# Attention over a graph: one merged exponential for each pair of tiles, scores in batches of three and five, x loaded in pieces

## The chip, the cores and the metric

The kernel runs on one core of a Trainium2 chip. The core has a matrix engine (PE, with its weight loads shown as PEld), a vector engine (DVE), a scalar engine (ACT), a general engine (POOL) and a queue engine that issues most transfers (SP). Matmul results go to a memory called PSUM, which this kernel uses as eight banks of 512 float32 columns. The metric is the device time of one launch in microseconds (us).

## The reference

Four graph layers run on x (3327 nodes, 128 features) and a 0/1 adjacency matrix adj (3327 x 3327). Each layer normalises, applies relu and adds its result to x. Cut to the layer that takes most of the time:

```python
h = jnp.maximum(_layernorm(x, axis=-1), 0.0)
q = (x @ Wq.T).reshape(d, n, h)      # x is h above; d = 128 heads, n = 3327 nodes, h = 8 elements
k = (x @ Wk.T).reshape(d, n, h)
v = (x @ Wv.T).reshape(d, n, h)
a = jnp.einsum('dnh,dmh->dnm', q, k) * scale
a = a + spatial_encoding + edge_encoding          # both are adj
a = jax.nn.softmax(a, axis=2)
out = jnp.einsum('dnm,dmh->dnh', a, v)
out = out.reshape(n, h * d)
return out @ Wo.T
```

So for each of 128 heads there are 3327 x 3327 scores of eight-element products, 2 adj is added, and the exponential of every score is needed: 1.4 thousand million exponentials. Layer 0 multiplies by adj twice, layer 2 is a gated unit on adj @ h, layer 3 picks nearest neighbours; all that lies outside the attention loop takes 1299 us of the span.

## The kernel before

**Tiling of the attention loop.** Query nodes lie in seven chunks of 476 columns (the last is shorter), key nodes in 26 tiles of 128 partitions (node = partition x 26 + tile), heads in 32 groups of four. A step is one key tile of one (chunk, group); there are 7 x 32 = 224 groups and 5824 steps. Two steps, an even tile and an odd tile, share one buffer `p8` of eight places of 476 columns, so there are 2912 pairs.

**One step, before (`scores`, lines 536 to 557).** Four score matmuls (line 547), one per head, each on its own 32 partitions of the array (their operands lie at partitions 32 i). The letters of `WAYS` (line 505) say how 2 adj reaches each score:

- D: the scores go to an "early" bank (four in turn), and DVE adds the tile of 2 adj while it copies them to `p8` (line 552).
- I: the scores go to a "late" bank, and a second matmul, of an identity with the tile of 2 adj (line 550), adds it in PSUM.
- G: the scores go to a late bank; ACT takes their exponential and POOL multiplies it by exp(2 adj), which is held for odd tiles (line 555).

The even tile is DDDI and the odd tile DDIG. ACT takes the exponential straight from the late banks (line 553): of one place in an even step and of two in an odd step. After the odd step it takes the exponential of the five D places of the pair at once, in place (line 557). PSUM is full: one bank for the accumulator, four early, one for `late1` and two for `late2`.

**Weighing (`weigh`, lines 559 to 576).** Four steps later (`ahead = 4`), four float32 matmuls, each in two passes, multiply the values (9 columns per head, the ninth being 1 for the softmax sum) by the exponentials and accumulate in `acc` (line 564). The four heads use four column groups of the array. After tile 25 DVE copies `acc` out (line 573), and the next group's first weighing may start after that.

**Order.** The loop stands under a manual schedule: each engine runs its instructions in the order of the program text. So PE runs scores, identity, weighing, step by step. A step also holds other work: at tile 4 the loads of the next group's heads on SP (`load_heads`, line 392), from tile 13 the casts of the keys on POOL (`key_pair`, line 414), and during the first chunk the parting of keys and queries into high and low parts on POOL (`Parting.at`). In the last group of a chunk ACT also takes the exponentials of the next chunk's adj tiles (`exp_of`). Outside this loop a planner orders instructions by costs of its own, so the order there need not be that of the text.

**Stage before the loop (lines 421 to 500).** For 26 blocks of nodes, q, k and v are projected on PE, copied by ACT to staging tiles and stored to DRAM from SP. Between blocks one entry of the list `early` runs (lines 444 to 457, line 478): parting of groups 0 and 1, all loads of the first heads in one entry, the exponentials for the first chunk in one entry, then two key casts in each entry. The staging tile of v comes from a pool of four and POOL writes a 1 into the ninth column before every use (line 473).

**Start.** x is loaded into `xs` (partition p holds nodes 26 p to 26 p + 25, called slots) by three transfers of whole rows, the split being in partitions (lines 95 to 98). The first layer norm works in three pieces of slots: `CUTS` (line 134) gives 0 to 4, 4 to 13 and 13 to 26.

Of the kernel before, what the change touches and what calls it, by code (L numbers as in the profile page):

```python
# [8 lines left out]
F32 = mybir.dt.float32  # L9
# [6 lines left out]
AF = mybir.ActivationFunctionType  # L16
# [33 lines left out]
def dram(ap, offset, dims):  # L50
    return bass.AP(tensor=ap.tensor, offset=ap.offset + offset, ap=dims)
# [3 lines left out]
def kernel(  # L55
# [38 lines left out]

    xs = const.tile([P, T, D], F32, name="xs")
    nc.vector.memset(xs[96:P, T - 1, :], 0.0)
    for p0, p1, n in ROW_PARTS:
        nc.sync.dma_start(xs[p0:p1, :n], dram(x_in, p0 * T * D, [[T * D, p1 - p0], [D, n], [1, D]]))

    weights = const  # L100

# [26 lines left out]
    def inv_sqrt(pool, src, name, scale=1.0, bias=0.0):  # L128
# [1 line left out]
        nc.scalar.activation(r, src, AF.Sqrt, bias=bias, scale=scale)  # L130
        nc.vector.reciprocal(r, r)
        return r

    CUTS = (0, T // 6, T // 2, T)

    def in_pieces(f, cuts=CUTS):

# [207 lines left out]
    def exp_of(a2, c):  # L345
        e = e_pool.tile([P, QW], F32, name="e")
        nc.scalar.activation(e[:, : even(c)], a2[:, : even(c)], AF.Exp)
        return e
# [40 lines left out]
                if t == 11:  # L389
                    self.store(side)  # L390

    def load_heads(c, g):
        q0, w = q_chunks[c]
        k_in = kq.tile([P, NP], F32, name="k_in", bufs=1)
        q4 = kq.tile([P, QW], F32R, name="q4")
        v4 = kq.tile([P, 4, T, EA], F32, name="v4")
        nc.gpsimd.memset(k_in[:, N:], 0.0)
        if w % 2:
            nc.gpsimd.memset(q4[:, w : w + 1].bitcast(F32), 0.0)
        for i in range(4):  # L400
            n0 = (4 * g + i) * N
            for j in range(2):
                r = 32 * i + HL * j
                nc.sync.dma_start(k_in[r : r + HL, :N], kt[:, n0 : n0 + N])
                nc.sync.dma_start(q4[r : r + HL, :w].bitcast(F32), dram(qt, E * j * GP + n0 + q0, [[0, 2], [GP, E], [1, w]]))
        for i in range(4):
            n0 = (4 * g + i) * N
            nc.sync.dma_start(
                v4[:, i].rearrange("p t e -> p (t e)"),
                vd[n0 : n0 + NP, :].rearrange("(p t) e -> p (t e)", t=T),  # L410
            )
        return k_in, q4, v4, []

    def key_pair(heads):
# [7 lines left out]
    with tc.tile_pool(name="l1", bufs=1) as pool, tc.tile_pool(name="l1_ps", bufs=3, space=PSUM) as ps:  # L422
# [22 lines left out]
        for g in range(2):  # L445
            part = Parting(g)
            for side in range(2):
                early.append(lambda part=part: (part.load(0), part.load(1)) if part.lo[0] is None else None)
                early.append(lambda part=part, side=side: [part.part(side, i) for i in range(4)] and part.store(side))
        first, e_first = [], []  # L450
        early.append(lambda: first.extend(load_heads(0, 0)))
        ahead_part = Parting(2)
        early.append(lambda: (ahead_part.load(0), ahead_part.load(1)))
        early.append(lambda: e_first.extend(exp_of(a, 0) for a in a_first[1::2]))
        early += [lambda: (key_pair(first), key_pair(first))] * (T // 4)
        if T // 2 % 2:
            early.append(lambda: key_pair(first))
        for r in range(T):
            kp = rows_of(r)
            lhs = hT[:, r * P : r * P + kp]  # L460
            for i, (dst, mx) in enumerate(((qf, q_max), (kf, k_max))):
                pp = ps.tile([P, 2, 512], F32, name="pp", bufs=2)
                for c in range(2):
                    nc.tensor.matmul(pp[:kp, c, :], lhs, w_st[:, i, c * 512 : c * 512 + 512], start=True, stop=True)
                s = st.tile([P, E * NH], F32, name="qk_st")
                nc.scalar.activation(s[:kp], pp[:kp].rearrange("p a b -> p (a b)"), AF.Copy, scale=D**-0.5 if i == 0 else 1.0)
                nc.vector.tensor_reduce(mx[:kp, r : r + 1], s[:kp], AX.X, ALU.max, apply_absolute_value=True)
                store(dst[:E].rearrange("e (r c) -> r e c", c=NH), s.rearrange("p (e c) -> p e c", c=NH), r, kp)
            pp = ps.tile([P, 2, 512], F32, name="pp", bufs=2)
            for c in range(2):  # L470
                nc.tensor.matmul(pp[:kp, c, :], lhs, w_st[:, 2, c * 512 : c * 512 + 512], start=True, stop=True)
            s = st.tile([P, NH, EA], F32, name="v_st")
            nc.gpsimd.memset(s[:, :, E : E + 1], 1.0)
            nc.scalar.copy(s[:kp, :, :E], pp[:kp].rearrange("p a (c e) -> p (a c) e", e=E))
            store(vd.rearrange("(r c) e -> r (c e)", c=NH), s.rearrange("p c e -> p (c e)"), r, kp)

            if r > 1 and early:
                early.pop(0)()
# [23 lines left out]

    WAYS = ("DDDI", "DDIG")
    PLACES = ((0, 1, 2, 5), (3, 4, 6, 7))
    two_i = const.tile([P, P], BF16, name="two_i")
    nc.vector.tensor_copy(two_i, ident)
    engines = {
# [9 lines left out]
    with tc.tile_pool(name="at_in", bufs=1) as a_pool, tc.tile_pool(name="at_p", bufs=3) as p_pool, tc.tile_pool(  # L519
# [13 lines left out]
            q0, w = q_chunks[c]  # L533
            nc.sync.dma_start(adj16[t][:, q0 : q0 + w], a2[:, :w])

        def scores(step, heads, a2, e_a, p8):
            c, _, t = step
            we = even(c)
            _, q4, _, pairs = heads
            ways, places = WAYS[t % 2], PLACES[t % 2]  # L540
            n_d = ways.count("D")
            late = ps.tile([P, 4 - n_d, 512], F32, name=f"late{4 - n_d}")
            early = [ps.tile([P, 512], F32, name="early", bufs=4) for _ in range(n_d)]
            for i in (*range(n_d, 4), *range(n_d)):
                r = slice(32 * i, 32 * i + 32)
                sp = early[i] if i < n_d else late[:, i - n_d]
                nc.tensor.matmul(sp[:, :we], pairs[t // 2][r, t % 2, :], q4[r, :we], start=True, stop=ways[i] != "I")  # L547
            for i in range(4):
                if ways[i] == "I":
                    nc.tensor.matmul(late[:, i - n_d, :we], two_i, a2[:, :we], start=False, stop=True)  # L550
            for i in range(n_d):
                nc.vector.tensor_tensor(p8[:, places[i], :we], early[i][:, :we], a2[:, :we], op=ALU.add)  # L552
            nc.scalar.activation(p8[:, places[n_d] : places[3] + 1, :we], late[:, :, :we], AF.Exp)  # L553
            if ways[3] == "G":
                nc.gpsimd.tensor_tensor(p8[:, places[3], :we], p8[:, places[3], :we], e_a[:, :we], op=ALU.mult)  # L555
            if t % 2:
                nc.scalar.activation(p8[:, :5, :we], p8[:, :5, :we], AF.Exp)  # L557

        def weigh(step, v4, p8):
            c, g, t = step  # L560
# [17 lines left out]
        with tc.manual_schedule(engines=engines):  # L578
# [7 lines left out]
            for j, step in enumerate(steps):  # L586
                c, g, t = step
                n = c * n_groups + g + 1
                more = n < len(groups)
                if t == 0 and j:  # L590
                    heads = coming
                    if g == 0:
                        a_t, a_next = a_next, []
                        e_t, e_next = e_next, []
                if t % 2 == 0:
                    p8 = p_pool.tile([P, 8, QW], F32, name="p8")
                scores(step, heads, a_t[t], e_t[t // 2], p8)
                begun[j] = (step, heads[2], p8)
                if j >= ahead:
                    weigh(*begun.pop(j - ahead))  # L600
                if t == min(4, T // 2) and more:
                    coming = load_heads(*groups[n])
                if c == 0 and g + 2 < n_groups:
                    if t == 0:
                        parting = ahead_part
                    for due in range(t, t + 1 if t < T - 1 else max(T, 16)):
                        parting.at(due)
                        if due == 15 and g + 3 < n_groups:
                            ahead_part = Parting(g + 3)
                            ahead_part.load(0)  # L610
                            ahead_part.load(1)

                if t >= T // 2 and more:
                    key_pair(coming)
                if t == min(6, T // 2) and c + 1 < len(q_chunks):
                    for _ in range(min(len(to_store), 1 + T // n_groups)):
                        store_adj(*to_store.pop(0))
                    a_in = [load_adj(c + 1, i) for i in range(len(a_next), T * (g + 1) // n_groups)]
                if t == max(T - 4, 3) and c + 1 < len(q_chunks):
                    for a, i, w in a_in:  # L620
                        a_next.append(doubled(adj_pools[(c + 1) % 2], a[: rows_of(i), :w], i, w))
                        to_store.append((c + 1, i, a_next[-1]))
                if t % 2 and g == n_groups - 1 and c + 1 < len(q_chunks):
                    e_next.append(exp_of(a_next[t], c + 1))
# [485 lines left out]
```

## Time and profile before

| | us |
|---|---|
| median of the runs (lowest, highest) | 11189.97 (11184.46, 11197.54) |
| the profiled execution's own time | 11195.14 |
| its span, first to last instruction | 11193.4 |
| PE busy | 10850.5 |
| ACT busy | 10199.3 |
| DVE busy | 9343.1 |
| POOL busy | 6016.3 |
| the attention loop, first to last exponential | 576.2 to 10470.6 |

A group line of the profile names the source line, engine, operation, what is written and read with its shape, and the count. After the first bar come the busy time in all and the mean in ns of one. After the second come the idle time of that engine just before these instructions and what ended most of it. Busy times of ACT and PE hold overlaps: an instruction is counted [...] while the next has already started. Where it matters the distance between starts is used; starts are taken from the trace's single records. A row of the timeline gives the start, the time covered, the engine, line and operation, and x for how many were merged into the row. In the table of stages each engine has its busy time with the count of instructions, then come the clock granted to PE, the share of the DMA engines and GB/s.

### The profile page before, as it was taken

How to read it: one execution, taken by the hardware profiler on the slowest of the kernel's cores; microseconds unless marked ns; L12 is line 12 of the kernel's file. 1: busy time of each engine (PE TensorE's matmuls, PEld its weight loads, DVE VectorE, ACT ScalarE, POOL GpSimd, SP SyncE). 2: the span in 40 equal slices, each digit the busy share in tenths (PEclk: the TensorE clock that was granted, in tenths of full speed). 3: DMA queues.
4: the chain of work that ended last, by engine and by line, in shares of the span. 5: the costliest groups of instructions: out<-in, count | busy, mean ns of one | idle time of the engine just before them, and what ended most of it. 6: DMA issues, size and time to landing. Idle time of an engine off the chain costs nothing. (4 is left out here: it accounts for less than half of the span.)

```text
span 11193.4 us, 209350 instructions
## 1 busy us (share of the span) xinstructions
PE 10850.5 (97%) x79530; PEld 3005.9 (27%) x79530; DVE 9343.1 (83%) x15429; ACT 10199.3 (91%) x9152; POOL 6016.3 (54%) x6964
## 2 busy tenths in 40 slices
PE   9899999999999999999999999999999999999996
PEld 4322222222222222222222222222222222222453
DVE  8588888888888888888888888888888888888656
ACT  0399999999999999999999999999999999999522
POOL 0277777555555555555555555555555555555203
PEclk9899999999999999999999999999999999999998
DMA  7755554333333333333333333333333332333432
GB/s 264 238 129 120 123 127 109 65 64 64 68 64 62 67 66 63 68 65 61 68 66 63 66 66 61 67 66 61 66 66 61 66 63 55 61 58 58 135 113 97
DMA packets 417541, 942.25 MB, mean 84 GB/s; under 512 B 67936, under 2 KB 345937, under 8 KB 380940
## 3 DMA queue, kind: packets, MB, share of 16 engines
q1 hardware_dynamic: 412762, 918.98, 37.4%
q8 instruction: 627, 10.27, 0.4%
q0 software_dynamic: 3760, 9.78, 0.3%
q14 instruction: 392, 3.21, 0.1%
HBM read 788.78 MB, written 139.71 MB: 83 GB/s over the span
## 5 line engine op out<-in xcount | busy, mean ns | idle before, releaser
L552 DVE TENSOR_TENSOR p<-early,a 128x476 f32<-128x476 f32 (+1 forms) x14560 | 8426.4, 646 | 1369.4 <-PE early L547 1297.5
L557 ACT ACTIVATE p<-p 128x2380 f32<-128x2380 f32 (+1 forms) x2912 | 7568.4, 2599 | 0.4
L564 PE MATMUL acc<-p,v 128*9 128x476 f32 (+1 forms) x46592 | 5748.5, 564 | 15.3 <-ACT p L557 1.4
L553 ACT ACTIVATE p<-late 128x476 f32<-128x476 f32 (+1 forms) x5824 | 5315.4, 1175 | 13.8 <-DMA q<-qt 10.2
L555 POOL TENSOR_TENSOR p<-p,e 128x476 f32<-128x476 f32 (+1 forms) x2912 | 3528.1, 1212 | 3204.3 <-ACT p L553 2998.6
L547 PE MATMUL late<-q,k 32*128 32x476 f32 (+1 forms) x8736 | 2798.2, 478 | 99.5 <-ACT p L553 39.7
L547 PE MATMUL early<-q,k 32*128 32x476 f32 (+1 forms) x14560 | 2843.6, 478 | 9.4 <-DVE p L552 9.4
L419 POOL CAST k<-k_in 128x256 fp32r<-128x256 f32 x2912 | 1936.5, 697 | 886.4 <-DMA k_in<-kt 339.4
L547 PEld LDWEIGHTS late<-q,k 32*128 32x128 f32 x8736 | 1065.4, 181 | 4890.4 <-ACT p L553 4186.2
L550 PE MATMUL late<-a,two_i 128*128 128x476 bf16 (+1 forms) x5824 | 2180.8, 374 | 0.0
L547 PEld LDWEIGHTS early<-q,k 32*128 32x128 f32 x14560 | 1113.0, 181 | 9.9 <-DVE p L552 9.9
L564 PEld LDWEIGHTS acc<-p,v 128*9 128x9 f32 x46592 | 695.2, 88 | 1272.6 <-issue 1185.8
L550 PEld LDWEIGHTS <-two_i 128*128 128x128 bf16 x5824 | 556.2, 96 | 1329.0 <-issue 1329.0
L189 ACT COPY agg<-agg_ps 128x512 f32<-128x512 f32 x15 | 8.2, 591 | 485.5 <-PE agg_ps L204 290.6
L230 PE MATMUL agg_ps<-a,part 128*128 128x512 bf16 (+1 forms) x1092 | 227.0, 369 | 4.3 <-ACT agg L928 3.2
L272 POOL TENSOR_SCALAR a<-a_in 128x476 bf16<-128x476 f32 (+2 forms) x156 | 221.1, 1417 | 0.5
L272 POOL TENSOR_SCALAR a<-a 128x476 bf16<-128x476 f32 (+1 forms) x26 | 36.4, 1400 | 288.1 <-DMA a<-in_adjT_dram 288.1
L923 PE MATMUL sp<-yT,hT 128*128 128x512 f32 (+1 forms) x364 | 170.7, 610 | 12.3 <-ACT agg L928 6.4
L204 PE MATMUL agg_ps<-a,h 128*128 128x512 f32 (+2 forms) x364 | 148.2, 570 | 26.2 <-DVE h L164 26.2
L573 DVE COPY o<-acc 105x476 f32<-105x476 f32 (+1 forms) x224 | 144.5, 645 | 4.6 <-PE acc L564 4.6
L204 PE MATMUL agg_ps<-a,x 128*128 128x512 f32 (+2 forms) x364 | 145.3, 562 | 0.6 <-ACT x L318 0.6
L230 PEld LDWEIGHTS <-part 128*128 128x128 f16 x1092 | 108.6, 99 | 117.7 <-issue 10.3
(236 smaller groups left out, 2592.0 us busy)
## 6 DMA issues: line engine op xcount, KB each, us to landing
k_in<-kt SPq DMA_DIRECT2D x1792, 207.9 KB
v<-vd SPq DMA_DIRECT2D x896, 117.0 KB
a<-in_adjT_dram SPq DMA_DIRECT2D x50, 1663.5 KB
a<-adj SPq DMA_DIRECT2D x78, 831.8 KB
q<-qt SPq DMA_DIRECT2D x1536, 29.8 KB
a_in<-in_adjT_dram SPq DMA_DIRECT2D x125, 238.0 KB
adj<-a SPq DMA_DIRECT2D x156, 119.0 KB
vd<-v_st SPq DMA_DIRECT2D x25, 576.0 KB
```

What stands on the lines that cost most here:

```text
L204: nc.tensor.matmul(acc[c][:, :w], lhs[:kp, t, :], a[:kp, c0 : c0 + w], start=(t == 0), stop=(t == T - 1))
L230: nc.tensor.matmul(acc[c][:, :w], part[:, t, :], a[:, c0 : c0 + w], start=(t == 0 and i == 0), stop=(t == T - 1 and i == len(parts) - 1),)
L272: nc.gpsimd.tensor_scalar(a2[:kp, :w], a, 2.0, None, op0=ALU.mult)
L419: nc.gpsimd.tensor_copy(k, slots(k_in)[:, t : t + 2, :])
L547: nc.tensor.matmul(sp[:, :we], pairs[t // 2][r, t % 2, :], q4[r, :we], start=True, stop=ways[i] != "I")
L550: nc.tensor.matmul(late[:, i - n_d, :we], two_i, a2[:, :we], start=False, stop=True)
L552: nc.vector.tensor_tensor(p8[:, places[i], :we], early[i][:, :we], a2[:, :we], op=ALU.add)
L553: nc.scalar.activation(p8[:, places[n_d] : places[3] + 1, :we], late[:, :, :we], AF.Exp)
L555: nc.gpsimd.tensor_tensor(p8[:, places[3], :we], p8[:, places[3], :we], e_a[:, :we], op=ALU.mult)
L557: nc.scalar.activation(p8[:, :5, :we], p8[:, :5, :we], AF.Exp)
L564: nc.tensor.matmul(acc[32 * i : 32 * i + EA, :w], v4[:kp, i, t, :], p8[:kp, PLACES[t % 2][i], :w], start=(t == 0), stop=(t == T - 1),)
L923: nc.tensor.matmul(sp[:, c0 : c0 + w], slots(zT)[:, t, :], z2T[:, cols], start=True, stop=False)
```

## The change

In the attention loop, `scores` is called once for a pair, at the even tile. Its eight score matmuls go out in two batches: heads 1, 2 and 3 of the even tile; then, after the weighing of an earlier even tile, head 0 of the even tile and heads 2, 3, 1 and 0 of the odd tile. Both identity matmuls follow the second batch. The one I place of the even tile is now head 0, and the three late places lie together in one tile of three banks, so that one activation takes their exponential (1428 columns); the exponential of the five D places follows it. In the odd step POOL multiplies (`times_e`), and the odd tile of the earlier pair is weighed.

Before the loop, the first heads' loads are split into eight pieces: four load keys and queries and run in entries of their own, four load values and run in the entries that cast keys, where the exponentials of the first chunk now stand as well. The four staging tiles of v are fixed ones, and their ninth column is set once.

At the start, x is loaded in three pieces of slots, eight transfers in all.

```diff
-    for p0, p1, n in ROW_PARTS:
-        nc.sync.dma_start(xs[p0:p1, :n], dram(x_in, p0 * T * D, [[T * D, p1 - p0], [D, n], [1, D]]))
+    CUTS = (0, T // 6, T // 2, T)
+    for t0, t1 in zip(CUTS, CUTS[1:]):
+        for p0, p1, n in ROW_PARTS:
+            m = min(t1, n) - t0
+            if m > 0:
+                nc.sync.dma_start(xs[p0:p1, t0 : t0 + m], dram(x_in, (p0 * T + t0) * D, [[T * D, p1 - p0], [D, m], [1, D]]))
...
-        first, e_first = [], []
-        early.append(lambda: first.extend(load_heads(0, 0)))
         ahead_part = Parting(2)
         early.append(lambda: (ahead_part.load(0), ahead_part.load(1)))
-        early.append(lambda: e_first.extend(exp_of(a, 0) for a in a_first[1::2]))
-        early += [lambda: (key_pair(first), key_pair(first))] * (T // 4)
-        if T // 2 % 2:
-            early.append(lambda: key_pair(first))
+        pieces, e_first = [], []
+        first = load_heads(0, 0, pieces)
+        early += pieces[:4]
+
+        key_steps = -(-(T // 2) // 2)
+        for i in range(key_steps):
+
+            def step(i=i):
+                for f in pieces[4 + i : 5 + i if i < key_steps - 1 else None]:
+                    f()
+                for n in (2 * i, 2 * i + 1):
+                    if n < T // 2:
+                        key_pair(first)
+                        e_first.append(exp_of(a_first[2 * n + 1], 0))
+
+            early.append(step)
+        v_sts = [st.tile([P, NH, EA], F32, name=f"v_st{i}", bufs=1) for i in range(4)]
+        for s in v_sts:
+            nc.gpsimd.memset(s[:, :, E : E + 1], 1.0)
...
-            s = st.tile([P, NH, EA], F32, name="v_st")
-            nc.gpsimd.memset(s[:, :, E : E + 1], 1.0)
+            s = v_sts[r % 4]
...
-    WAYS = ("DDDI", "DDIG")
-    PLACES = ((0, 1, 2, 5), (3, 4, 6, 7))
+    WAYS = ("IDDD", "DDIG")
+    PLACES = ((5, 0, 1, 2), (3, 4, 6, 7))
+
+    BATCHES = (((0, 1), (0, 2), (0, 3)), ((0, 0), (1, 2), (1, 3), (1, 1), (1, 0)))
...
+        def scores(step, heads, a2s, between):
+
+            c, _, t = step
+            we = even(c)
+            _, q4, _, pairs = heads
+            p8 = p_pool.tile([P, 8, QW], F32, name="p8")
+            late = ps.tile([P, 3, 512], F32, name="late")
+            for n, batch in enumerate(BATCHES):
+                if n == 1:
+                    between()
+                for odd, i in batch:
+                    way, place = WAYS[odd][i], PLACES[odd][i]
+                    sp = ps.tile([P, 512], F32, name="early", bufs=4) if way == "D" else late[:, place - 5]
+                    r = slice(32 * i, 32 * i + 32)
+                    nc.tensor.matmul(sp[:, :we], pairs[t // 2][r, odd, :], q4[r, :we], start=True, stop=way != "I")
+                    if way == "D":
+                        nc.vector.tensor_tensor(p8[:, place, :we], sp[:, :we], a2s[odd][:, :we], op=ALU.add)
+            for odd, i in BATCHES[1]:
+                if WAYS[odd][i] == "I":
+                    nc.tensor.matmul(late[:, PLACES[odd][i] - 5, :we], two_i, a2s[odd][:, :we], start=False, stop=True)
+            nc.scalar.activation(p8[:, 5:, :we], late[:, :, :we], AF.Exp)
+            nc.scalar.activation(p8[:, :5, :we], p8[:, :5, :we], AF.Exp)
+            return p8
+
+        def times_e(step, p8, e_a):
+            we = even(step[0])
+            assert WAYS[1][3] == "G"
+            nc.gpsimd.tensor_tensor(p8[:, PLACES[1][3], :we], p8[:, PLACES[1][3], :we], e_a[:, :we], op=ALU.mult)
...
                 if t % 2 == 0:
-                    p8 = p_pool.tile([P, 8, QW], F32, name="p8")
-                scores(step, heads, a_t[t], e_t[t // 2], p8)
+                    p8 = scores(step, heads, a_t[t : t + 2], lambda: weigh(*begun.pop(j - ahead)) if j >= ahead else None)
+                else:
+                    times_e(step, p8, e_t[t // 2])
+                    if j >= ahead:
+                        weigh(*begun.pop(j - ahead))
                 begun[j] = (step, heads[2], p8)
-                if j >= ahead:
-                    weigh(*begun.pop(j - ahead))
```

More of the change, by code (lines that the diff above doesn't have):

```diff
@@ L132, in inv_sqrt @@
         return r
-    CUTS = (0, T // 6, T // 2, T)
     def in_pieces(f, cuts=CUTS):
@@ L390, in at, with load_heads @@
                     self.store(side)
-    def load_heads(c, g):
+    def load_heads(c, g, pieces=None):
         q0, w = q_chunks[c]
@@ L399, in load_heads, with scored @@
             nc.gpsimd.memset(q4[:, w : w + 1].bitcast(F32), 0.0)
-        for i in range(4):
+        def scored(i):
             n0 = (4 * g + i) * N
@@ L405, in load_heads, with weighted @@
                 nc.sync.dma_start(q4[r : r + HL, :w].bitcast(F32), dram(qt, E * j * GP + n0 + q0, [[0, 2], [GP, E], [1, w]]))
-        for i in range(4):
+        def weighted(i):
             n0 = (4 * g + i) * N
@@ L411, in load_heads @@
             )
+        for f in (scored, weighted):
+            for i in range(4):
+                if pieces is None:
+                    f(i)
+                else:
+                    pieces.append(lambda f=f, i=i: f(i))
         return k_in, q4, v4, []
@@ L447 @@
             for side in range(2):
-                early.append(lambda part=part: (part.load(0), part.load(1)) if part.lo[0] is None else None)
+                if side == 0:
+                    early.append(lambda part=part: (part.load(0), part.load(1)))
                 early.append(lambda part=part, side=side: [part.part(side, i) for i in range(4)] and part.store(side))
-        first, e_first = [], []
-        early.append(lambda: first.extend(load_heads(0, 0)))
         ahead_part = Parting(2)
         early.append(lambda: (ahead_part.load(0), ahead_part.load(1)))
-        early.append(lambda: e_first.extend(exp_of(a, 0) for a in a_first[1::2]))
-        early += [lambda: (key_pair(first), key_pair(first))] * (T // 4)
-        if T // 2 % 2:
-            early.append(lambda: key_pair(first))
+        pieces, e_first = [], []
[14 more added lines that the diff above has]
+            nc.gpsimd.memset(s[:, :, E : E + 1], 1.0)
         for r in range(T):
@@ L534, in store_adj @@
             nc.sync.dma_start(adj16[t][:, q0 : q0 + w], a2[:, :w])
-        def scores(step, heads, a2, e_a, p8):
+        def scores(step, heads, a2s, between):
             c, _, t = step
@@ L539, in scores @@
             _, q4, _, pairs = heads
[L540 to L555, printed above, removed]
@@ L556, in scores @@
-            if t % 2:
-                nc.scalar.activation(p8[:, :5, :we], p8[:, :5, :we], AF.Exp)
+            p8 = p_pool.tile([P, 8, QW], F32, name="p8")
[10 more added lines that the diff above has]
+                        nc.vector.tensor_tensor(p8[:, place, :we], sp[:, :we], a2s[odd][:, :we], op=ALU.add)
@@ L595 @@
                 if t % 2 == 0:
-                    p8 = p_pool.tile([P, 8, QW], F32, name="p8")
-                scores(step, heads, a_t[t], e_t[t // 2], p8)
+                    p8 = scores(step, heads, a_t[t : t + 2], lambda: weigh(*begun.pop(j - ahead)) if j >= ahead else None)
+                else:
+                    times_e(step, p8, e_t[t // 2])
+                    if j >= ahead:
+                        weigh(*begun.pop(j - ahead))
                 begun[j] = (step, heads[2], p8)
-                if j >= ahead:
-                    weigh(*begun.pop(j - ahead))
                 if t == min(4, T // 2) and more:
```

## The prediction

> **What bounds the kernel now.** I read the page first, then the stages, then the attention loop one instruction at a time.
>
> ```profile
> PE 10850.5 (97%) x79530; PEld 3005.9 (27%) x79530; DVE 9343.1 (83%) x15429; ACT 10199.3 (91%) x9152; POOL 6016.3 (54%) x6964
> ...
> L552 DVE TENSOR_TENSOR p<-early,a 128x476 f32<-128x476 f32 (+1 forms) x14560 | 8426.4, 646 | 1369.4 <-PE early L547 1297.5
> L557 ACT ACTIVATE p<-p 128x2380 f32<-128x2380 f32 (+1 forms) x2912 | 7568.4, 2599 | 0.4
> L564 PE MATMUL acc<-p,v 128*9 128x476 f32 (+1 forms) x46592 | 5748.5, 564 | 15.3 <-ACT p L557 1.4
> L553 ACT ACTIVATE p<-late 128x476 f32<-128x476 f32 (+1 forms) x5824 | 5315.4, 1175 | 13.8 <-DMA q<-qt 10.2
> L547 PEld LDWEIGHTS late<-q,k 32*128 32x128 f32 x8736 | 1065.4, 181 | 4890.4 <-ACT p L553 4186.2
> ```
>
> Two engines look full. The stage table separates them: in the middle of the loop ACT has no gap.
>
> ```profile
> 4000.00:6000.00 2000.00, 1978.30 (x15305) 486.30 (x15301) 1726.38 (x2988) 2000.00 (x1780) 1127.07 (x1258) 1.00 0.34 65
> ```
>
> Here the columns are PE, PEld, DVE, ACT, POOL. PE's busy time is no verdict, because ends are modelled; starts tell more. The timeline of ACT, then of PE:
>
> ```profile
> 5003.34 1.79 ACT L553 ACTIVATE p<-late 128x476 f32<-128x476 f32 x2
> 5004.63 2.57 ACT L557 ACTIVATE p<-p 128x2380 f32<-128x2380 f32 x1
> 5006.71 1.80 ACT L553 ACTIVATE p<-late 128x476 f32<-128x476 f32 x2
> ```
> ```profile
> 5004.40 0.48 PE L547 MATMUL late<-q,k 32*128 32x476 f32 x1
> ...
> 5004.81 0.37 PE L550 MATMUL late<-a,two_i 128*128 128x476 bf16 x1
> 5005.12 0.99 PE L564 MATMUL acc<-p,v 128*9 128x476 f32 x8
> 5006.03 0.48 PE L547 MATMUL late<-q,k 32*128 32x476 f32 x2
> ```
>
> One pair of tiles takes ACT 6.71 - 3.34 = 3.37 us. Over the loop the mean steps from start to start are 0.448 us (one late row of 476), 0.854 (two, 952; median 0.844) and 2.083 (the five, 2380), together 3.384. With the slope between the first two, 0.396/476 = 0.832 ns an element, each instruction costs its elements and only 0.05 to 0.10 us more: the durations 0.996, 1.403 and 2.626 overlap. 2912 pairs x 3.384 + 78 exponentials of the next chunk x 0.488 = 9892 us, against 9894 from first to last exponential (576.2 to 10470.6). So ACT sets the loop.
>
> PE comes close behind. Medians of its starts: scores to identity 0.419, identity to weighing 0.305, weighing to the next scores 0.917, so 1.641 per tile or 3.282 per pair. The tile following an odd one starts 1.743 later: 0.10 us of waiting for ACT per pair. That 0.10 is all the cover PE has.
>
> **What the skill says.** The Trainium skill, "ScalarE: Activation LUTs", What ACT_TABLE_LOAD costs: an activation with immediates takes 186 ns + 0.833 N, and neighbours overlap by 93 ns, so one instruction fewer would be worth some 93 ns. The trace agrees on the slope, but the two late ones show only 0.05. "TensorEngine Tiling (Array Packing)", Key Properties: changing the tiling mode drains TensorE, while separate tiles run in parallel. The trace agrees: four score matmuls start within 0.010 us, and each switch of shape leaves about 0.1 us beyond streaming. "TensorE: Matmul & The Clock Gate", LDWEIGHTS: columns / 1.2 ns, so 107 ns for 128 columns. This fits the 0.419: 0.010 of dispatch, 0.107 weight load in the open after the switch, 476 columns 0.200 (L230's matmuls of 512 columns start 0.216 apart), about 0.102 drain. The same page, Part 3, says weight loads overlap a running matmul only where the row group differs. This trace shows otherwise for L927:
>
> ```profile
> 10839.14 0.12 PEld L927 LDWEIGHTS <-one_rows 3*128 3x128 bf16 x6 [0.23 <-issue]
> 10839.14 0.61 PE L927 MATMUL sp<-n_rows,one_rows 3*128 3x512 bf16 x6
> ```
>
> Six weight loads lie within 0.12 us, though these are two rounds on the same three row groups; the second round's matmuls start 0.227 after the first (10839.143, 10839.370), which is 512 columns (0.213) and little else.
>
> **The change, part by part.**
>
> *Merged exponential.* ACT loses one start per pair: 0.448 + 0.854 become 1428 x 0.8333 + 0.05 = 1.240, plus 0.010 of present waits. ACT's pair becomes 1.250 + 2.083 = 3.333, a saving of 0.051, or 149 us over 2912 pairs if ACT stayed the bound.
>
> *Batches of three and five.* The eight scores and two identity products of a pair (L550, x5824, one per tile) remain, the identities now back to back. The order on PE is: three scores (even heads 1 to 3), weigh, five scores, two identities, weigh. The five are four row groups and then a fifth, odd head 0, on the group of even head 0, so it streams after it. New sum, in start-to-start steps:
> - three scores to weighing: 0.419 less two dispatch steps of 0.0035 = 0.412. The switch from 32-row straight to 9-column shape is in no row; I price it as the one to the identity. Bounds 0.30 (weights loaded ahead, no drain beyond 0.1) to 0.45.
> - weighing to the five: 0.917.
> - five scores to identity: 0.107 + 0.200 + 0.200 + 0.010 + 0.099 = 0.616, with the fifth's weights loaded under the first, as at L927. If not, 0.723.
> - two identities: 0.305 + 0.200 = 0.505; the second needs no switch.
> - weighing: 0.917.
>
> Together 3.367, against 3.282 before: the added serial pass costs more than the merged identity switch returns. PE's 3.367 now lies above ACT's 3.333, so PE becomes the bound and its own waits count in full.
>
> *Where a group of 26 tiles begins.* The accumulator is copied out by DVE after tile 25 is weighed, and the next group's first weighing waits for it.
>
> ```profile
> 5007.86 0.64 DVE L573 COPY o<-acc 105x476 f32<-105x476 f32 x1
> ...
> 5008.12 0.38 PE L550 MATMUL late<-a,two_i 128*128 128x476 bf16 x1
> ...
> 5008.55 0.12 PEld L564 LDWEIGHTS acc<-p,v 128*9 128x9 f32 x8 [0.34 <-DVE o L573]
> ```
>
> Today scores and identity (0.724) lie between; PE loses 5008.55 - 5008.12 - 0.305 = 0.13 of its cover. Then only three scores (0.412) lie between. Last pass at 0.43 after the weighing's start, modelled end 0.99, about 0.08 to DVE, copy 0.64, 0.05 back: 1.77 against 0.917 + 0.412 = 1.33, so 0.44 us. Queued behind: both batches' scores, hence the adds and the exponentials. The first tile of a group also staggers its scores on the new heads' loads (+0.185, median of groups); I keep that (0 if those waits are taken ahead).
>
> A group: 13 x 3.367 + 0.44 + 0.185 = 44.40, against 44.14 measured now. In the 6 of 224 groups that carry 13 extra exponentials ACT stays the bound and gains 13 x 0.051 = 0.7. Loop: 218 x 0.26 - 4 = +53.
>
> *POOL's multiplication* moves to the odd step, before that tile's weighing, in the same order on POOL. It must be done two pairs later (6.7 us) and takes 1.21. *Adds on DVE*: five of 0.56 start to start, 2.8 of 3.37. Both cost nothing; the cover is 0.5 us per pair on DVE.
>
> *Heads in pieces, value buffers set once.* The projection stage stalls around the first load of heads:
>
> ```profile
> 477.08 1.01 ACT L474 COPY v_st<-pp 128x1024 f32<-128x1024 f32 x1 [2.41 <-PE pp L471]
> 496.17 1.02 ACT L466 ACTIVATE qk_st<-pp 128x1024 f32<-128x1024 f32 x1 [18.07 <-DMA qf<-qk_st]
> ```
>
> SP stands in 16 head loads and 4 value loads from 471 to 491 while the stores of results queue behind. Spread over eleven row blocks, each 4 loads cost SP about 2 us per 5.15 us block, and POOL's casts no longer hold the value buffers' memsets. The DMA engines are full (share 1.0) after 500 us and 0.85 to 0.9 before, so at most 15 us come back; I take -10 (bounds -18 to +5).
>
> *x in pieces.* Eight issues for three, about 0.4 us each on SP, under a transfer of 1.7 MB. DVE's first reduction waits elsewhere:
>
> ```profile
> 12.60 0.28 POOL masks.py:199 TENSOR_SCALAR_AFFINE_SELECT ident<-ident 128x128 f32<-128x128 f32 x1 [10.49 <-issue]
> ...
> 12.91 0.23 DVE L508 CAST two_i<-ident 128x128 bf16<-128x128 f32 x1 [11.43 <-POOL ident masks.py:199]
> ```
>
> The cast stands ahead of it on DVE. I take 0; -8 if the planner now puts the layer norm first, +2 if adj's loads start later.
>
> Sum: +53 - 10 = +43 on the span of 11193.4; the profiled run was 11195.1 and the median of the runs is 11190, so 11233.
>
> **Rivals.**
> - *The fifth score shows its weight load.* For it: the skill's sentence. Against: L927. Price 0.107 x 2834 pairs = +303: 11536.
> - *The new switch is cheap, ACT stays the bound (faster).* The place is three scores to weighing. For: never seen, may load weights early; against: every switch in the trace costs about 0.1. Break-even with today is a pair of 3.352, only 0.015 below my sum; below 3.344 it is faster. Below 3.285 ACT decides, for the full -149 - 10: 11031.
> - *A tie at today's time.* The stagger at group starts is taken ahead and the switch is 0.005 cheaper: about 11190.
>
> **How the numbers follow.** Forecast 0.60 (of it 0.05 faster, 0.15 within, 0.40 slower; own range 11160 to 11310), weight load in the open 0.13, cheap switch 0.22, tie 0.05. 0.2% is 22 us, about what a measurement of this kernel can tell from no change. Faster 0.05 + 0.22 = 0.27; same 0.15 + 0.05 = 0.20; slower 0.40 + 0.13 = 0.53. Range 11070 to 11380: it leaves out the open weight load and the far end of the cheap switch.
>
> **What would show it.** Right: PE's starts between even-tile scores 3.36 to 3.40 apart, 0.6 from first of the five to the identity, ACT with small gaps before the late exponential, 128x1428, started 1.24 before the five's. Wrong: ACT without gaps at 3.33 (cheap switch), or 0.72 and more in the five (open load or slower passes); a first layer norm before 12 us.

## The result, and the profile after

The changed kernel takes 11281.08 us (median; 11280.3 to 11284.58) against 11189.22 for the kernel before: a ratio of 1.0082, 95% interval 1.0066 to 1.0098, so 0.8% slower. The forecast was 11233, slower, with 11070 to 11380 as its range.

The profiled spans, 11193.4 and 11280.1, split as follows (us):

| stage | before | after | difference |
|---|---|---|---|
| start to the first exponential of five | 579.1 | 566.9 | -12.2 |
| attention loop, first to last exponential of five | 9891.5 | 9994.7 | +103.3 |
| all after it | 722.8 | 718.5 | -4.3 |

The code of the last stage is the same in both. It took 716.3 to 723.0 in the ten experiments, so 4 us are no more than it varies from run to run.

The page of the changed kernel, parts 1, 4 and 5:

```profile
PE 10972.7 (97%) x79530; PEld 3043.5 (27%) x79530; DVE 9357.5 (83%) x15429; ACT 10188.3 (90%) x6240; POOL 6011.7 (53%) x6942
...
PE 89%; ACT 5%; DVE 2%; issue 2%; DMA 1%; POOL 1%; SPq 0%; DVEq 0%; ACTq 0%; POOLq 0%
...
L584 ACT ACTIVATE p<-p 128x2380 f32<-128x2380 f32 (+1 forms) x2912 | 6348.7, 2180 | 0.0
...
L583 ACT ACTIVATE p<-late 128x1428 f32<-128x1428 f32 (+1 forms) x2912 | 3965.8, 1362 | 129.4 <-PE late L582 122.8
```

ACT lost 2912 instructions (9152 to 6240) and now has gaps before the late exponential, where it waits for PE's identity: 129 us in all, where it had 14. The exponentials of the five are recorded with 2180 ns on the mean instead of 2599 although they do the same work. Records of ACT are longer in the kernel before, where its loop has no gaps, so its busy total (10199 to 10188) does not show the saving. The chain that ended last is PE for 89% of the span. For the kernel before the same view held only the last microseconds and named no engine above 0%.

ACT's timeline, and PE's, in the middle of the loop:

```profile
5003.49 1.36 ACT L583 ACTIVATE p<-late 128x1428 f32<-128x1428 f32 x1
5004.75 2.18 ACT L584 ACTIVATE p<-p 128x2380 f32<-128x2380 f32 x1
5006.87 1.36 ACT L583 ACTIVATE p<-late 128x1428 f32<-128x1428 f32 x1
```
```profile
5004.22 0.49 PE L577 MATMUL early<-q,k 32*128 32x476 f32 x3
5004.64 0.99 PE L597 MATMUL acc<-p,v 128*9 128x476 f32 x8
5005.56 0.48 PE L577 MATMUL late<-q,k 32*128 32x476 f32 x3
5005.56 0.68 PE L577 MATMUL early<-q,k 32*128 32x476 f32 x2
5006.18 0.57 PE L582 MATMUL late<-a,two_i 128*128 128x476 bf16 x2
5006.68 0.99 PE L597 MATMUL acc<-p,v 128*9 128x476 f32 x8
5007.60 0.49 PE L577 MATMUL early<-q,k 32*128 32x476 f32 x3
```

The pair takes PE 7.60 - 4.22 = 3.38 us. The row of two early scores covers 0.68, where a row of scores that run side by side covers 0.48 or 0.49: the fifth score starts 0.322 (median) after the first of its batch.

The timeline at the start of a group:

```profile
5041.47 0.48 PE L577 MATMUL early<-q,k 32*128 32x476 f32 x3
5041.63 0.65 DVE L606 COPY o<-acc 105x476 f32<-105x476 f32 x1
...
5042.34 0.22 PEld L597 LDWEIGHTS acc<-p,v 128*9 128x9 f32 x8 [0.69 <-DVE o L606]
...
5043.35 0.19 PEld L577 LDWEIGHTS late<-q,k 32*128 32x128 f32 x3 [0.80 <-issue]
```

From the three scores to the weighing it takes 0.87 us instead of 0.42, and the next scores follow the weighing after 1.01 instead of 0.92: together 0.55 us a group. Before, such a group began with a wait of 0.13, and that was inside PE's slack.

The timelines at the start of the program:

```profile
3.68 0.69 DVE L159 TENSOR_REDUCE ln_mean<-xs 128x4 f32<-128x512 f32 x1 [2.19 <-DMA xs<-in_x_dram]
...
14.09 19.00 PE L206 MATMUL agg_ps<-a,h 128*128 128x512 f32 x42 [14.09 <-DVE ln_mean L159]
37.61 22.63 PE L206 MATMUL agg_ps<-a,h 128*128 128x512 f32 x50 [4.53 <-DMA a<-in_adjT_dram]
```

The planner now puts the first piece of the layer norm ahead of the cast that waits for POOL. PE starts 12 us earlier (14.09 for 26.16), then waits 4.5 us for adj: the fourth tile is loaded only when DVE, which is in the layer norm's later pieces until then, has released the first of three buffers (its copy from there ends at 31.20, SP issues the load at 31.27). At the end of the first layer 6.0 of the 12 us are left (ACT's first copy of the second product at 334.88 instead of 340.90); the projection stage adds 6.2.

### The profile page after: what moved, and what is told of

Same layout as the page of the kernel before. It is cut to its first block, busy times and chain, and to the rows that moved or that the text cites. A ratio compares the mean times of both kernels' runs of the same rounds, so it can differ in the third digit from the quotient of the medians.

```text
span 11280.1 us, 206623 instructions
## 1 busy us (share of the span) xinstructions
PE 10972.7 (97%) x79530; PEld 3043.5 (27%) x79530; DVE 9357.5 (83%) x15429; ACT 10188.3 (90%) x6240; POOL 6011.7 (53%) x6942
## 4 chain that ended last, share of the span: by engine, by line
PE 89%; ACT 5%; DVE 2%; issue 2%; DMA 1%; POOL 1%; SPq 0%; DVEq 0%; ACTq 0%; POOLq 0%
PE acc L597 45%; PE early L577 15%; PE late L582 12%; PE late L577 10%; PE agg_ps L206 2%; ACT p L584 2%; ACT p L583 2%; PE agg_ps L232 1%; DVE o L606 1%; PE pp L490 1%; DMA qf<-qk_st 0%; POOL rows L988 0%; ACT e L349 0%; PE yp L772 0%; PE pp L497 0%
## 5 line engine op out<-in xcount | busy, mean ns | idle before, releaser
L584 ACT ACTIVATE p<-p 128x2380 f32<-128x2380 f32 (+1 forms) x2912 | 6348.7, 2180 | 0.0
L583 ACT ACTIVATE p<-late 128x1428 f32<-128x1428 f32 (+1 forms) x2912 | 3965.8, 1362 | 129.4 <-PE late L582 122.8
L577 PE MATMUL early<-q,k 32*128 32x476 f32 (+1 forms) x14560 | 3414.1, 457 | 11.4 <-DVE p L579 10.3
L577 PEld LDWEIGHTS early<-q,k 32*128 32x128 f32 x14560 | 1372.5, 182 | 2334.6 <-DVE p L579 2329.1
L582 PE MATMUL late<-a,two_i 128*128 128x476 bf16 (+1 forms) x5824 | 1675.1, 369 | 0.0
L577 PE MATMUL late<-q,k 32*128 32x476 f32 (+1 forms) x8736 | 1415.8, 479 | 22.6 <-ACT p L583 22.5
L577 PEld LDWEIGHTS late<-q,k 32*128 32x128 f32 x8736 | 547.3, 181 | 2345.8 <-ACT p L583 2168.1
L582 PEld LDWEIGHTS <-two_i 128*128 128x128 bf16 x5824 | 330.7, 97 | 965.0 <-issue 965.0
```

Of the source, the lines that this page charges most:

```text
L577: nc.tensor.matmul(sp[:, :we], pairs[t // 2][r, odd, :], q4[r, :we], start=True, stop=way != "I")
L582: nc.tensor.matmul(late[:, PLACES[odd][i] - 5, :we], two_i, a2s[odd][:, :we], start=False, stop=True)
L583: nc.scalar.activation(p8[:, 5:, :we], late[:, :, :we], AF.Exp)
```

## The experiments

Theory: PE has become the bound of the loop, by the serial fifth score and the wait at group starts; what the merge saves on ACT cannot be used. Rivals: the part ahead of the loop disturbs the loop; ACT is still the bound; the loss lies in the wait at group starts alone. All diffs are against the changed kernel, and cut. In the expectations TensorE is PE, VectorE is DVE, ScalarE is ACT and GpSimd is POOL.

**The two halves of the change apart.** First the loop of before, whole, with the new part ahead of it:

```diff
-    WAYS = ("IDDD", "DDIG")
-    PLACES = ((5, 0, 1, 2), (3, 4, 6, 7))
-    BATCHES = (((0, 1), (0, 2), (0, 3)), ((0, 0), (1, 2), (1, 3), (1, 1), (1, 0)))
+    WAYS = ("DDDI", "DDIG")
+    PLACES = ((0, 1, 2, 5), (3, 4, 6, 7))
...
-            nc.scalar.activation(p8[:, 5:, :we], late[:, :, :we], AF.Exp)
+            nc.scalar.activation(p8[:, places[n_d] : places[3] + 1, :we], late[:, :, :we], AF.Exp)
```

> The loop of before with all that the change does ahead of it (x in pieces, heads in pieces, value buffers set once). Theory: the first exponential of five came at 566.9 us instead of 579.1 in the changed kernel, and the loop of before keeps its 3.398 us per pair, so some 12 us less than before: 11177 (11170 to 11182). Rival: the earlier start is lost again in the loop's first groups, which wait for parted keys: 11189.

Measured 11176.82, ratio 0.9991 (0.9982 to 0.9999) to before; first exponential of five at 566.0 and 3.396 us a pair. Then the reverse, the new loop with all that is ahead of it as before (x, the heads' loads and the value tiles):

```diff
-    CUTS = (0, T // 6, T // 2, T)
-    for t0, t1 in zip(CUTS, CUTS[1:]):
-        for p0, p1, n in ROW_PARTS:
...
+    for p0, p1, n in ROW_PARTS:
+        nc.sync.dma_start(xs[p0:p1, :n], dram(x_in, p0 * T * D, [[T * D, p1 - p0], [D, n], [1, D]]))
...
-        first = load_heads(0, 0, pieces)
...
+        early.append(lambda: first.extend(load_heads(0, 0)))
```

> The loop of after with the head of before. Theory: the loss is all in the loop (103 us from the first to the last exponential of five), so about 12 us more than the changed kernel: 11293 (11285 to 11300). Rival: moving loads and casts ahead of the loop disturbed the loop, and it runs like before without them: 11190.

Measured 11290.75, ratio 1.0093 (1.0077 to 1.0108); loop 9992.6, as in the changed kernel. The loss is all in the loop, and the rest of the change gains some 10 us: 11.4 from the kernel before to the first of these runs, 9.7 from the second to the changed kernel.

**The fifth score left out.** Odd head 0 is not computed; its add reads head 1's scores.

```diff
+                    fifth = (odd, i) == (1, 0)
+                    if not fifth:
-                    sp = ps.tile(...)
+                        sp = ps.tile(...)
...
-                    nc.tensor.matmul(...)
+                    if not fifth:
+                        nc.tensor.matmul(...)
```

> Leaves out the score matmul of odd head 0, the fifth of the second batch; its add reads the scores of odd head 1 instead, so DVE, ACT and POOL do the same work. Theory (TensorE sets the loop, and the fifth pass is what pushed it past ScalarE): TensorE's pair falls from 3.379 to 3.17 us, ScalarE takes over at 3.333, a group takes 43.4 instead of 44.47, 218 groups: about -230, 11050 (11020 to 11090). Rival (ScalarE still sets the loop, TensorE's waits are harmless): 11281, no change.

Measured 11003.54, ratio 0.9835. The page of this run:

```profile
L587 ACT ACTIVATE p<-p 128x2380 f32<-128x2380 f32 (+1 forms) x2912 | 7455.6, 2560 | 1.4 <-DVE p L582 1.4
...
L586 ACT ACTIVATE p<-late 128x1428 f32<-128x1428 f32 (+1 forms) x2912 | 5025.0, 1726 | 13.0 <-DMA k_in<-kt 10.6
```

One of 26 matmul records in a pair, 0.2 us on PE, is worth 278 us: ACT's gaps fall from 129 us to 13, its records are long again, and its period is 3.317 (median), the ACT floor of the merged form. Before, the floor was 3.369. A group takes 43.20 us, of which 13 x 3.317 = 43.12: with slack on PE the wait at group starts nearly vanishes, as the expectation had counted. The gain lies above the expected range because ACT's floor is 3.317 and not 3.333: 13 x 0.016 x 218 = 45 us. The run also fills one early bank less in a pair. That is not what it gains by: no step of the changed kernel's PE shows a wait for a bank. Its scores follow the weighing after 0.917 us (median) as in the kernel before, and its fifth score starts where the weight load and the streaming put it (0.322, see below). So PE was the bound, and the merge does save 0.052 us a pair where ACT can use it.

**The wait at group starts taken away.** DVE copies a piece of x in place of the accumulator, so PE need not wait, and the attention result is not stored.

```diff
-                nc.vector.tensor_copy(o4[: 96 + EA, :w], acc[: 96 + EA, :w])
+                nc.vector.tensor_copy(o4[: 96 + EA, :w], xs.rearrange("p t d -> p (t d)")[: 96 + EA, :w])
```

> Leaves out the copy of the accumulator: VectorE copies a piece of x instead at the same place, so TensorE does not wait for it at the start of a group; the attention result is not stored. Theory: the second pair of a group loses its extra 0.55 us (3.934 against 3.38), 218 groups: -120, 11160 (11140 to 11180). Rival (the wait is absorbed, because ScalarE catches up in it): 11275 to 11281.

Measured 11157.66, ratio 0.9973 (0.9961 to 0.9985). The wait costs 123 us in a loop bound by PE, more than the whole loss of 92. So the last rival is right on where the time is lost: outside group starts a pair takes 3.38 us in the changed kernel and took as much before (43.99 / 13 = 3.384), so what the loop loses, 103 us, it loses at its group starts (0.55 x 218 = 120, less 14 for pairs shorter by 0.005 and 4 in the six longer groups). They cost that much because the fifth score has used up PE's slack: without that score the same wait leaves 0.08 us a group.

**The batches without the merge.**

```diff
-            late = ps.tile([P, 3, 512], F32, name="late")
+            late1 = ps.tile([P, 1, 512], F32, name="late1")
+            late2 = ps.tile([P, 2, 512], F32, name="late2")
...
-            nc.scalar.activation(p8[:, 5:, :we], late[:, :, :we], AF.Exp)
+            nc.scalar.activation(p8[:, 5:6, :we], late1[:, :, :we], AF.Exp)
+            nc.scalar.activation(p8[:, 6:, :we], late2[:, :, :we], AF.Exp)
```

> The batches of three and five without the merged exponential: the late scores lie in a tile of one bank and a tile of two, with an activation each. Theory (TensorE sets the loop, so what the merge saves on ScalarE buys nothing there): 11281 to 11310. Rival (ScalarE still sets the loop): the merge's 0.052 us per pair is missing, 2834 pairs: 11430.

Measured 11288.85, ratio 1.0085 (1.0068 to 1.0102), which cannot be told from the changed kernel. With these batches the merge is worth nothing that can be measured; without the fifth pass it would be worth, as an estimate, up to 0.052 x 2834 = 147 us.

**The merge in the order of before.** All four even heads first, then all four odd ones:

```diff
-    BATCHES = (((0, 1), (0, 2), (0, 3)), ((0, 0), (1, 2), (1, 3), (1, 1), (1, 0)))
+    BATCHES = (((0, 0), (0, 1), (0, 2), (0, 3)), ((1, 2), (1, 3), (1, 1), (1, 0)))
```

> The merged exponential with the batches in the order of before: all four heads of the even tile, then all four of the odd tile, identities after the second. No fifth pass. Theory: even head 0 needs the late bank at the start of a pair, and that is released only when the merged exponential has read it, some 2.04 us after the identities of the pair before (0.63 to its start, 1.36 long, 0.05); then 0.42 + 0.917 + 0.42 to the next identities: pair 3.80, so about 12360 (12200 to 12500). Rival (the bank is free in time): 11003.

Measured 12646.29 in one run, above the expected range; 3.874 us a pair where 3.80 was expected. PE in the timeline:

```profile
5004.45 0.47 PE L577 MATMUL late<-q,k 32*128 32x476 f32 x1 [0.62 <-ACT p L583]
```

Every pair waits 0.6 us until the merged exponential has left the late bank. So with three late scores in one tile a late score in the first batch brings this wait. If only the three D scores of the even tile go there, five remain for four row groups: the fifth pass is the price of the merge in this order, and the next run shows what another order costs.

**Four and four, with D scores first.** Odd head 0 moves up:

```diff
-    BATCHES = (((0, 1), (0, 2), (0, 3)), ((0, 0), (1, 2), (1, 3), (1, 1), (1, 0)))
+    BATCHES = (((0, 1), (0, 2), (0, 3), (1, 0)), ((0, 0), (1, 2), (1, 3), (1, 1)))
```

> Odd head 0 moves from the second batch to the first: two batches of four, four row groups each, no fifth pass, nothing left out. Theory: TensorE's own sum falls to 3.17 us per pair, but the first batch now needs all four early banks, and the last of the five adds on VectorE ends some 3.56 us after the batch started (0.60 to the first add, four steps of 0.566, 0.645, 0.05): pair 3.36, between ScalarE's 3.32 and the changed kernel's 3.38; with the wait at group starts about 11210 (11140 to 11250). Rival (the fifth pass was all, banks are free in time): like the run without it, 11003.

Measured 11195.76, ratio 1.0004 (0.9995 to 1.0012) to before, 85 us less than the changed kernel. Pairs alternate between 3.318 and 3.41, mean 3.365. PE's timeline, then DVE's:

```profile
5008.13 0.85 PE L577 MATMUL early<-q,k 32*128 32x476 f32 x4
```
```profile
5005.55 2.89 DVE L579 TENSOR_TENSOR p<-early,a 128x476 f32<-128x476 f32 x5 [0.72 <-PE early L577]
```

The four scores, else 0.49, stretch over 0.85: the fourth waits until the fifth add ends at 5.55 + 2.89 = 8.44. The fifth pass has turned into a wait for the last early bank, as expected in place and size. A late fourth score delays the rest of its pair, and then the bank is free in time for the next: hence every second pair.

**Both tiles weighed together.** Four and four, both weighings between the batches, the accumulator's copy after the second batch:

```diff
-                    p8 = scores(step, heads, a_t[t : t + 2], lambda: weigh(*begun.pop(j - ahead)) if j >= ahead else None)
+                    done = [begun.pop(i) for i in (j - ahead, j - ahead + 1) if i >= 0]
+                    p8 = scores(step, heads, a_t[t : t + 2], lambda: [weigh(*d) for d in done])
+                    for d in done:
+                        copy_out(d[0])
```

> Two batches of four as in the run before, and both tiles of the earlier pair are weighed together between the batches, so the array changes its shape four times a pair instead of five; the accumulator's copy is issued after the second batch's adds. Nothing is left out. Theory (TensorE's sum and the wait for the last early bank set the four-four version): own sum 0.417 + 1.73 + 0.42 + 0.505 = 3.07 us, with the bank wait (3.56 + 0.41 + 2.655) / 2 = 3.31, so ScalarE's 3.317 takes over: like the run without the fifth pass, 11003 (10990 to 11060). Rival: the weighed tiles are needed about 1.4 us earlier, and the exponentials or GpSimd's product are late for it (slack by my sum 0.4 us): 11150 or more.

Measured 11305.95, ratio 1.0101 (1.0084 to 1.0117): a miss, and not by the rival's way. PE and DVE of this run:

```profile
5008.49 1.96 DVE L579 TENSOR_TENSOR p<-early,a 128x476 f32<-128x476 f32 x3
...
5009.24 0.48 PE L577 MATMUL early<-q,k 32*128 32x476 f32 x1
...
5010.15 0.82 PE L577 MATMUL early<-q,k 32*128 32x476 f32 x4
5010.91 1.39 PE L597 MATMUL acc<-p,v 128*9 128x476 f32 x12
```

The same wait has moved. The second batch now comes so late (5009.23) that its own D score, not the four adds ahead, sets the fifth add, the last of the DVE row (single records: 5009.79 to 5010.45); the next batch's fourth score waits 0.35 us for it every pair, and the pair is 3.40. With the batches of three and five:

```diff
-    BATCHES = (((0, 1), (0, 2), (0, 3), (1, 0)), ((0, 0), (1, 2), (1, 3), (1, 1)))
+    BATCHES = (((0, 1), (0, 2), (0, 3)), ((0, 0), (1, 2), (1, 3), (1, 1), (1, 0)))
```

> The changed kernel's batches of three and five, with both earlier tiles weighed together between them. Theory: one change of shape less takes TensorE's sum to 3.28 us, but the next batch of three now comes 1.1 us after the five, and its third score waits for the bank of the first of the five's two adds: pair (3.86 + 2.87) / 2 = 3.365, about 11190 (11140 to 11230). Rival (the change of shape is all): ScalarE's 3.317, 11003.

Measured 11433.18, ratio 1.0215 (1.0194 to 1.0235): also a miss. Pairs take 3.40, and the second pair of a group 4.21, where the copy now stands behind the second batch's adds (it starts 1.63 after the weighing's end, where it took 0.10 in the changed kernel). Between groups the change of shape that is saved returns as a wait for a bank: three scores to weighing are 0.55 instead of 0.42.

**One add for two heads.** Four and four, with even heads 1 and 2 in a tile of two banks, two single banks for the other D scores, and even head 3 first:

```diff
-    BATCHES = (((0, 1), (0, 2), (0, 3)), ((0, 0), (1, 2), (1, 3), (1, 1), (1, 0)))
+    BATCHES = (((0, 3), (0, 1), (0, 2), (1, 0)), ((0, 0), (1, 2), (1, 3), (1, 1)))
...
+                    if (odd, i) == (0, 1):
+                        early2 = ps.tile([P, 2, 512], F32, name="early2")
...
+                    if (odd, i) == (0, 2):
+                        nc.vector.tensor_tensor(
+                            p8[:, 0:2, :we], early2[:, :, :we], a2s[0][:, :we].unsqueeze(1).to_broadcast([P, 2, we]), op=ALU.add
+                        )
```

> The two batches of four once more, with even heads 1 and 2 in one early tile of two banks and one add for both; the other D scores share two single banks. Nothing is left out. Theory: in the four-four run the fourth score of a batch waits for the last of five adds, 0.61 + 4 x 0.566 + 0.65 + 0.05 = 3.57 us after the batch before; one add of 952 elements for two of 476 saves a start (some 0.07), so the wait is shorter by that and the pair, whose period takes half of it, goes from 3.366 to about 3.335, near ScalarE's 3.317: 13 x 0.03 x 218 = -85, about 11115 (11080 to 11160). Rival (an add of two banks costs twice one, or the single banks come too late): 11196 or more.

Measured 11114.69, ratio 0.9934 (0.9918 to 0.9951) to before: faster than both kernels, with nothing left out. A group line of its page:

```profile
L585 DVE TENSOR_TENSOR p<-early,a 128x952 f32<-128x952 f32 (+1 forms) x2912 | 3316.1, 1139 | 0.0
```

An add of 952 elements is followed 1.06 us later, two of 476 take 2 x 0.561 (medians). Pairs alternate between 3.317 and 3.35. The chain to the last bank is shorter by the 0.07 that the sum gave it.

## Why the prediction was right, and where its sum was off

The outcome, slower, and its mechanism were right, shown by the run without the fifth score (PE was the bound) and by the batches alone (the merge buys nothing). The signs named for it came: 3.38 us between even tiles' scores, 0.63 from the five to the identity, small gaps on ACT before the late exponential. The size was less than half: +43 forecast, +92 measured. Term by term:

- *TensorE's pair.* Forecast 3.367; medians after: three scores to weighing 0.417 (forecast 0.412), weighing 0.917 (0.917), five to identity 0.628 (0.616), identities 0.505 (0.505), weighing 0.917 (0.917). For the three scores the forecast took off two dispatch steps of 0.0035, where three scores have one step fewer than four. Outside group starts a pair takes 3.379 on the mean. The switch from 32-row to 9-column shape, which no row had shown, cost what the other switches cost, so the rival that made it cheap fell. The fifth score started 0.322 after the first, against 0.107 + 0.200 + 0.010 = 0.317: its weights were loaded under the running matmul (the trace has the load from 5005.662 to 5005.846, the first score's matmul from 5005.555 to 5006.034), and the rival with the open load fell with it. The sentence of the Trainium skill, "TensorE: Matmul & The Clock Gate", Part 3, that weight loads overlap matmuls in flight only when the row group differs does not hold for this run; the same part also lets a load go ahead when it targets the background weight buffer, and no run here shows which buffer was used. The 0.012 is worth 13 x 0.012 x 218 = +34 us.
- *Group starts.* Forecast 0.44 for the copy and 0.185 for the stagger, measured 0.55. The copy's wait is 0.45, the weighing after it loses 0.10, and the stagger at a group's first scores does not show in the periods. -16 us. That the 0.55 counts in full is shown by the run without the wait: 0.55 x 218 = 120, measured 123.
- *The base of comparison* was wrong. The 44.14 us of a group before is about the mean over all groups (9891.5 / 224 = 44.16), with the six that carry 13 extra exponentials (50.2 each); it was set against 218 groups without them, whose mean is 43.99. 0.15 x 218 = +33 us. Those six gained 0.69 each, as forecast 0.7.
- *Sum for the loop:* 53 + 34 - 16 + 33 = 104, measured 103.
- *Ahead of the loop.* Forecast -10 for the projection and 0 for x, measured -6.2 and -6.0. For x the planner did put the layer norm first, which the text had as its lower bound (-8); a first layer norm before 12 us, named as a sign of being wrong, came at 3.68. In the nine experiments with the same code ahead of the loop the first exponential of five came between 566.0 and 570.0, so each share is known to a few us only. And x takes nine transfers (L102 in the trace), not eight.
- *ACT.* Forecast 3.333 as its floor, measured 3.317 in the run without the fifth score; the saving of 0.051 was 0.052.

## What to carry to other kernels

Before relieving the bound engine, write down how far the next one is behind: here PE had 0.10 us of cover in a pair of 3.38, and a merge worth 0.05 was bought with 0.2 of serial work on PE. When two engines are this close, waits that slack had hidden are paid in full at once (0.13 hidden became, with less work of PE to cover it, 0.55 paid per group), and a bank's release chain can be the next bound; count the chain from the first producer to the last release, as the four-four runs did. When groups of a loop differ in kind, compare like with like: a mean that holds six longer groups of 224 cost this forecast 33 us, where its loop came out 50 too low.

## What was not expected of the hardware

The same activation of 128x2380 is recorded with 2.18 us on the mean in the changed kernel, whose ACT has gaps, and with 2.56 to 2.60 where ACT has none (the kernel before, its loop with the new part ahead, and the run without the fifth score), though the next start follows after 2.08 in each, gaps taken off; busy time fell by 11 us while 2912 instructions went. A gap just before is not what decides: in the four-four run half of the pairs follow without one and are recorded with 2.19. What the longer records hold is not shown. Two add instructions merged into one over two PSUM banks save 0.07 us, and this, with the order and the banks changed along with it, was worth some 80 us of 11196.
